# Gated units: the short chunk of the inner dimension in both halves of the rows, its product for four tiles on quarters of the array

## The chip, the cores and the metric

One Trainium2 chip, one of its cores. The metric is the device time of one execution in microseconds, median of several. A profiled execution, recorded by the hardware profiler, gives the trace that is read below. Engines: PE is TensorE (PEld its weight loads), DVE is VectorE, ACT is ScalarE, POOL is GpSimd, SP is the queue that issues most DMAs.

## The reference

Input x has 2 batches of 2048 tokens with 256 channels, all float32. Two blocks, each wrapped as `x + layernorm(block(layernorm(x)))`. The first is a sparse attention with compressed, selected and windowed parts. The second, which the change touches, is two layers of local attention, each followed by gated units:

```python
x = x + o @ wo                                    # after the local attention
h = shift_token(x)                                # second half of the channels from the token before
h = (h - mu) / jnp.sqrt(var + 1e-05) * lg + lb
h = h @ w1 + b1                                   # 256 -> 2 * 682
a, g = jnp.split(h, 2, axis=-1)
h = a * jax.nn.gelu(g, approximate=False)
x = x + h @ w2 + b2                               # 682 -> 256
```

The inner dimension is 682 = 5 * 128 + 42. After layer 1 comes the closing: layer norm of the result, plus the residual, to the output.

## The kernel before

Tokens are worked in tiles of 128; four tiles are a group (`GT = 4`), and there are eight groups, taken in the order `GORDER`. `Y[g]` holds a group's tokens in SBUF, `X[g]` the outer residual. The gated units of a layer are in `gated_units`. For each group:

- `shift` (DMA) makes the shifted half of the channels in `sh`; `moments` (DVE) and `deviations` (POOL) give mean and reciprocal deviation; `normed` (DVE) writes eight normalised 128x128 pieces into `hh`.
- `second_bias` adds b2 to the whole group on POOL, in place.
- `turned` (two of them, for the two halves of the channels) transposes four tiles on PE into a bank `pc`, and DVE writes them back with scale and bias as `hT`, also part of `hh`.
- `inner` multiplies one chunk c of the inner dimension for all four tiles: 512 columns, gate part into a bank `pg` and linear part into `pu`. The chunks 0 to 4 have 128 rows; chunk 5, the short one, has 42 (`REST`), and its gate and linear parts share one bank, gate rows at partitions 0 to 41 and linear rows at 64 to 105.
- `gate` applies Gelu on ACT into `ge`, and DVE multiplies into `u[:, c, :]`. There are two buffers u.
- `back` multiplies a tile's six chunks of u by w2 into a `pc` bank of 128x256 and adds it to Y on DVE. Chunk 5 is multiplied over all 128 rows; rows beyond 42 of u and w2 are zero.
- in the last layer `closing_moments` (DVE, then POOL for the reciprocal deviation r) and `closing_norm` (DVE norm to `res`, POOL adds X, SP stores) for each tile.

PSUM has 8 banks here, `share(ctx, "psum2", pa=2, pb=2, pc=4)`. A bank is reused in turn, when its last reader is done.

The order of the work is written by hand: `put(place, f, ...)` notes an operation with a place, and all are issued sorted by place, each engine taking its instructions in that order. `inner` of chunk c of the i-th group stands at (6 i + c) steps (`STEP`), so a place of 6 + k of a group is chunk k of the next one. `back` of tile k stands at 6 + k, `closing_moments` at 6.5 + k, `closing_norm` at 7.5 + k; `turned` at -2.1 and -1.1, that is in chunks 3.9 and 4.9 of the group before; `second_bias` at -2.5; `shift` at -9. So while a group's chunks are multiplied, the previous group's back products and the next group's norm and turns lie between them. A float32 product is two instructions in the trace. All of the gated units' instructions have the line of the recording helper, L124.

`Vectors.load` loads bias rows that are turned to columns (`col`); `load_gated` loads w1, w2 and b2 of a layer.

Of the kernel before, what the change touches and what calls it, by code (L numbers as in the profile page):

```python
# [12 lines left out]
AF = mybir.ActivationFunctionType  # L13
ALU = mybir.AluOpType
AX = mybir.AxisListType

P = 128
B, L, H = 2, 2048, 256
NT = L // P
GT = 4  # L20
# [4 lines left out]
HALF = 64  # L25
# [3 lines left out]
DEPTH, HEADS, DH = 2, 8, 64  # L29
INNER = HEADS * DH  # L30
HID = int(H * 4 * 2 / 3)
NCH = -(-HID // P)
FULL = (NCH - 1) * P
REST = HID - FULL
# [119 lines left out]
def sandwich_kernel(ctx: ExitStack, tc: tile.TileContext, x, Wq, bq, Wk, bk, Wv, bv, Wo, bo, Wg, bg,  # L154
                    Wc, bc, Ws, bs, wqkv, q_scale, k_scale, wo, ln_g, ln_b, w1, b1, w2, b2, rope, out):
    nc = Notes(tc.nc)
# [24 lines left out]
    def pc(shape):  # L181
        return bank("pc", shape)
# [10 lines left out]
    Y = [const.tile([P, GT, H], F32, tag=f"Y{g}", name=f"Y{g}") for g in range(B * NG)]  # L193
# [6 lines left out]
    def load(dst, src):  # L200
        nc.cut()
        nc.sync.dma_start(dst, src)
# [23 lines left out]
    cols = {}  # L226

    class Vectors:
# [10 lines left out]
        def load(self):  # L239
            if any(n % P for _, _, n in self.parts):  # L240
                nc.gpsimd.memset(self.row, 0.0)
            r = 0
            for _, src, n in self.parts:
                full = n // P
                load(self.row[r : r + full, :], src[0 : full * P].rearrange("(r p) -> r p", p=P))
                if n % P:
                    load(self.row[r + full : r + full + 1, 0 : n % P], src[full * P : n].unsqueeze(0))
                r += -(-n // P)

        def turn(self):  # L250
# [6 lines left out]
        (f"b1a{l}", b1[l, 0:HID], HID), (f"b1g{l}", b1[l, HID : 2 * HID], HID),  # L257
        (f"lg{l}", ln_g[l], H), (f"lb{l}", ln_b[l], H))])

    def col(name, i, n=P):  # L260
        return cols[name, i][:n]


    wpool = ctx.enter_context(tc.tile_pool(name="wpool", bufs=1))
# [33 lines left out]
    with part1 as s1:  # L298
# [403 lines left out]
        W = [dict() for _ in PAIRS]  # L702
# [186 lines left out]
    def load_gated(l):  # L889
        b2_b = wf.tile([P, H], F32, tag="b2", name=f"b2{l}")  # L890
        nc.gpsimd.dma_start(b2_b, b2[l].unsqueeze(0).to_broadcast([P, H]))


        a = wf.tile([P, 2, W1C], F32, tag="w1", name=f"w1{l}")
        w1v = w1[l].rearrange("(h p) n -> p h n", p=P)
        nc.gpsimd.memset(a[:, :, 2 * FULL :], 0.0)
        nc.sync.dma_start(a[:, :, 0:FULL], w1v[:, :, 0:FULL])
        nc.sync.dma_start(a[:, :, FULL : 2 * FULL], w1v[:, :, HID : HID + FULL])
        nc.sync.dma_start(a[:, :, 2 * FULL : 2 * FULL + REST], w1v[:, :, HID + FULL : 2 * HID])
        nc.sync.dma_start(a[:, :, 2 * FULL + HALF : 2 * FULL + HALF + REST], w1v[:, :, FULL:HID])  # L900
        o = wf.tile([P, NCH, H], F32, tag="w2", name=f"w2{l}")
        nc.gpsimd.memset(o[:, NCH - 1, :], 0.0)
        nc.sync.dma_start(o[:, 0 : NCH - 1, :], w2[l, 0:FULL, :].rearrange("(c p) n -> p c n", p=P))
        nc.sync.dma_start(o[0:REST, NCH - 1, :], w2[l, FULL:HID, :])
        return a, o, b2_b


# [6 lines left out]
    W = [dict() for _ in range(DEPTH)]  # L914
# [271 lines left out]
    GORDER = [b * NG + j for j in range(NG) for b in range(B)]  # L1186
# [6 lines left out]
    def gated_units(l, base, no_gate_until, beside):  # L1193
        G = {g: dict(u=U[i % 2]) for i, g in enumerate(GORDER)}

        def shift(g):

            s, y = G[g], Y[g]
            sh = act.tile([P, GT, P], F32, tag="oT", name="sh")
            if g % NG:  # L1200
                nc.sync.dma_start(sh[0:1, 0, :], G[g - 1]["kept"][P - 1 : P, :])
            else:
                nc.gpsimd.memset(sh[0:1, 0, :], 0.0)
            nc.sync.dma_start(sh[0:1, 1:GT, :], y[P - 1 : P, 0 : GT - 1, P:H])
            nc.sync.dma_start(sh[1:P, :, :], y[0 : P - 1, :, P:H])
            s["kept"] = act.tile([P, P], F32, tag="kept", name="kept", bufs=3)
            nc.gpsimd.tensor_copy(s["kept"], y[:, GT - 1, P:H])
            s["sh"] = sh

        def moments(g, k):  # L1210
            s = G[g]
            if k == 0:
                s["mv"] = small.tile([P, GT, 2], F32, tag="mv4", name="mv")
            stats(s["mv"][:, k, :], Y[g][:, k, 0:P], s["sh"][:, k, :])

        def deviations(g):
            G[g]["r"] = rstd_of(G[g]["mv"], GT, 1e-5)

        def normed(g, h, k):
            s = G[g]  # L1220
            if "hn" not in s:
                hh = act.tile([P, 2, 2 * GT * P], F32, tag="rr", name="hh")
                s["hn"] = hh[:, 0].rearrange("p (h k t) -> p h k t", h=2, k=GT)
                s["hT"] = hh[:, 1].rearrange("p (h t) -> p h t", h=2)
            norm(s["hn"][:, h, k, :], s["sh"][:, k, :] if h else Y[g][:, k, 0:P], s["mv"], k, s["r"])

        def second_bias(g):
            nc.gpsimd.tensor_tensor(Y[g], Y[g], W[l]["b2"].unsqueeze(1).to_broadcast([P, GT, H]), ALU.add)

        def turned(g, h):  # L1230
            s = G[g]
            pt = pc([P, GT, P])
            for k in range(GT):
                nc.tensor.transpose(pt[:, k, :], s["hn"][:, h, k, :], ident)
            nc.vector.tensor_scalar(s["hT"][:, h, :], pt.rearrange("p k t -> p (k t)"), col(f"lg{l}", h),
                                    col(f"lb{l}", h), ALU.mult, ALU.add)

        def inner(g, c, gate_bank, bank):
            s, w1_s = G[g], W[l]["w1"]

            def project(ps, lo):
                for h in range(2):
                    nc.tensor.matmul(ps, lhsT=w1_s[:, h, lo : lo + P], rhs=s["hT"][:, h, :],
                                     start=(h == 0), stop=(h == 1))

            pg = gate_bank([P, GT * P])
            if c < NCH - 1:
                pu = bank([P, GT * P])
                project(pg, FULL + c * P)
                project(pu, c * P)  # L1250
            else:
                pu = pg[HALF : HALF + REST]
                project(pg, 2 * FULL)
            s["in", c] = pg, pu

        def gate(g, c):
            s = G[g]
            pg, pu = s["in", c]
            n = P if c < NCH - 1 else REST
            ge = act.tile([P, GT * P], F32, tag="sq", name="ge")  # L1260
            nc.scalar.activation(ge[:n], pg[:n], AF.Gelu, bias=col(f"b1g{l}", c, n))
            nc.vector.scalar_tensor_tensor(s["u"][:n, c, :], pu[:n], col(f"b1a{l}", c, n), ge[:n],
                                           ALU.add, ALU.mult)

        def back(g, k):
            s, y = G[g], Y[g]
            pz = pc([P, H])
            for c in range(NCH):
                nc.tensor.matmul(pz, lhsT=s["u"][:, c, k * P : (k + 1) * P], rhs=W[l]["w2"][:, c, :],
                                 start=(c == 0), stop=(c == NCH - 1))  # L1270
            nc.vector.tensor_tensor(y[:, k, :], pz, y[:, k, :], ALU.add)

        def closing_moments(g, k):
            mv = small.tile([P, 1, 2], F32, tag="mv1", name="mv")
            stats(mv[:, 0, :], Y[g][:, k, :])
            G[g]["close", k] = mv, rstd_of(mv, 1, 1e-5)

        def closing_norm(g, k):
            res = act.tile([P, H], F32, tag="res", name="res")
            mv, r = G[g]["close", k]  # L1280
            norm(res, Y[g][:, k, :], mv, 0, r)
            nc.gpsimd.tensor_tensor(res, res, X[g][:, k, :], ALU.add)
            row = (g * GT + k) * P
            nc.sync.dma_start(of[row : row + P, :], res)


        plan = [(NCH + k, back, k) for k in range(GT)]
        plan += [(-9, shift), (-6, deviations), (-2.5, second_bias), (-2.1, turned, 0), (-1.1, turned, 1)]
        plan += [(-7 + 0.22 * k, moments, k) for k in range(GT)]
        plan += [(-4.5 + 0.22 * (h * GT + k), normed, h, k) for h in range(2) for k in range(GT)]  # L1290
        if l == DEPTH - 1:
            plan += [(NCH + k + 0.5, closing_moments, k) for k in range(GT)]
            plan += [(NCH + k + 1.5, closing_norm, k) for k in range(GT)]
        for i, g in enumerate(GORDER):
            for c in range(NCH):
                place = base + (NCH * i + c) * STEP
                put(place, inner, g, c, pc if place > beside else pa, pb if no_gate_until < place < beside else pc)
                put(max(place, no_gate_until) + 10, gate, g, c)
            for at, f, *arg in plan:
                put(base + (NCH * i + at) * STEP + 20, f, g, *arg)  # L1300

    def fetch(l, what):
# [75 lines left out]
```

## Time and profile before

| | us |
|---|---|
| median of 3 runs | 1618.66 (1618.02 to 1618.82) |
| profiled execution, its own time | 1617.42 |
| its span, first to last instruction | 1615.7 |
| PE busy | 1530.9 |
| DVE busy | 1068.0 |
| ACT busy | 757.3 |
| POOL busy | 733.5 |
| layer 0's gated units, about | 671 to 965 |
| layer 1's gated units, about | 1347 to 1612 |
| mean granted PE clock | 0.976 of full speed |

Times in the views are microseconds from the start of the span. A row of the timeline gives start, length, engine, line, operation, output and inputs, shape and count, and in brackets how long the engine had been idle and what released it. A row of the table of windows gives the stretch, its length, busy time of PE, PEld, DVE, ACT and POOL with instruction counts, the granted clock, the DMA share and GB/s.

### The profile page before, as it was taken

How to read it: one execution, taken by the hardware profiler on the slowest of the kernel's cores; microseconds unless marked ns; L12 is line 12 of the kernel's file. 1: busy time of each engine (PE TensorE's matmuls, PEld its weight loads, DVE VectorE, ACT ScalarE, POOL GpSimd, SP SyncE). 2: the span in 40 equal slices, each digit the busy share in tenths (PEclk: the TensorE clock that was granted, in tenths of full speed). 3: DMA queues.
4: the chain of work that ended last, by engine and by line, in shares of the span. 5: the costliest groups of instructions: out<-in, count | busy, mean ns of one | idle time of the engine just before them, and what ended most of it. 6: DMA issues, size and time to landing. Idle time of an engine off the chain costs nothing.

```text
span 1615.7 us, 32188 instructions
## 1 busy us (share of the span) xinstructions
PE 1530.9 (95%) x12216; PEld 1013.0 (63%) x12216; DVE 1068.0 (66%) x3123; ACT 757.3 (47%) x2197; POOL 733.5 (45%) x906
## 2 busy tenths in 40 slices
PE   7999957999999999789999999999999987999998
PEld 6867743666666666546566556666666664656655
DVE  6588673788888888544445247888888884455543
ACT  5236652677676776411111147677676763111110
POOL 7114255666666666301111156666666661132332
PEclk9999987999999999899999999999999998999999
DMA  6000002000000000020000010000000000000000
GB/s 213 1 4 4 1 2 80 8 5 8 6 8 9 5 7 7 8 68 7 10 20 0 1 39 28 9 5 9 5 8 8 9 4 9 11 25 28 27 26 26
DMA packets 32389, 30.66 MB, mean 19 GB/s; under 512 B 5118, under 2 KB 30572, under 8 KB 32236
## 3 DMA queue, kind: packets, MB, share of 16 engines
q1 hardware_dynamic: 32044, 28.08, 5.7%
q8 instruction: 97, 1.59, 0.4%
q0 software_dynamic: 192, 0.52, 0.2%
q14 instruction: 56, 0.46, 0.1%
HBM read 20.21 MB, written 4.19 MB: 15 GB/s over the span
## 4 chain that ended last, share of the span: by engine, by line
PE 87%; DVE 5%; POOL 3%; DMA 3%; ACT 1%; issue 1%; SPq 0%; POOLq 0%; DVEq 0%; ACTq 0%
PE pa L124 30%; PE pb L124 23%; PE pc L124 23%; PE pa L150 5%; PE pc L150 3%; DMA sh<-Y 2%; PE pb L150 2%; PE po L150 1%; DVE prob L124 1%; POOL rr L124 1%; DVE rr L124 1%; DVE st L150 1%; POOL r L150 1%; DMA cs<-in_rope_dram 0%; POOL ss L124 0%
## 5 line engine op out<-in xcount | busy, mean ns | idle before, releaser
L124 PE MATMUL pa<-wqkv,h 128*128 128x512 f32 x768 | 377.6, 615 | 19.3 <-ACT h L124 9.9
L124 POOL TENSOR_TENSOR rr<-rr 128x256 f32<-128x256 f32 x256 | 178.0, 727 | 305.8 <-DVE rr L124 259.4
L124 ACT ACTIVATE ge<-pa,vb 128x512 f32<-128x512 f32 x92 | 63.1, 688 | 365.7 <-PE pa L124 360.3
L124 ACT ACTIVATE prob<-prob,off 128x192 f32<-128x192 f32 (+2 forms) x512 | 226.2, 445 | 11.9 <-DVE off L124 11.0
L124 PEld LDWEIGHTS pa<-wqkv,h 128*128 128x128 f32 x768 | 133.9, 194 | 134.7 <-issue 107.7
L124 POOL TENSOR_TENSOR ss<-ss,mhalf 128x16 f32<-128x16 f32 x64 | 188.0, 2937 | 3.3 <-DVE den L124 2.3
L124 ACT COPY probT<-pb 128x384 f32<-128x384 f32 (+1 forms) x256 | 119.9, 469 | 142.6 <-PE pb L124 139.6
L124 PE MATMUL pa<-hh,w 128*128 128x512 f32 x368 | 176.4, 609 | 5.3 <-ACT ge L124 5.3
L124 PE MATMUL pc<-w,u 128*128 128x256 f32 x768 | 175.7, 379 | 0.0
L124 PEld LDWEIGHTS pc<-w,u 128*128 128x128 f32 x768 | 145.8, 190 | 45.4 <-issue 28.7
L124 DVE CUSTOM_DVE_ANT_0 prob<-pc,mask_loc 128x192 f32<-128x192 f32 (+2 forms) x512 | 148.7, 346 | 25.9 <-PE pc L124 24.1
L124 DVE TENSOR_TENSOR rr<-pa,cs 128x1024 f32<-128x1024 f32 x128 | 150.6, 1216 | 21.6 <-POOL cs L124 14.0
L124 PE MATMUL pb<-hh,w 128*128 128x512 f32 x292 | 137.7, 594 | 0.0
L124 POOL TENSOR_SCALAR r<-mv 128x1 f32<-128x1 f32 (+1 forms) x48 | 11.2, 233 | 274.9 <-DVE mv L124 274.9
L124 POOL TENSOR_TENSOR rr<-rr,ss 128x512 f32<-128x512 f32 x128 | 132.9, 1058 | 2.3
L124 DVE TENSOR_TENSOR prob<-prob,den 128x768 f32<-128x768 f32 x128 | 128.0, 1000 | 4.9
L124 PE MATMUL pb<-wo,oT 128*128 128x256 f32 x512 | 124.8, 388 | 5.8 <-DVE oT L124 5.8
L124 PEld LDWEIGHTS pb<-ident,prob 128*128 128x128 f32 x752 | 89.2, 141 | 65.4 <-DVE prob L124 27.7
L124 PE MATMUL pb<-ident,prob 128*128 128x128 f32 x752 | 118.3, 279 | 11.2 <-DVE prob L124 9.4
L124 DVE SCALAR_TENSOR_TENSOR u<-pb,vb,ge 128x512 f32<-128x512 f32 x73 | 54.7, 750 | 105.6 <-PE pb L124 79.8
L124 ACT ACTIVATE sq<-pa 128x512 f32<-128x512 f32 x128 | 75.9, 593 | 97.0 <-PE pa L124 94.2
L124 PE MATMUL pc<-kr,qT 64*64 64x192 f32 (+2 forms) x2688 | 111.1, 289 | 3.4 <-ACT qT L124 3.4
(255 smaller groups left out, 2498.6 us busy)
## 6 DMA issues: line engine op xcount, KB each, us to landing
cs<-in_rope_dram SPq DMA_DIRECT2D x32, 128.0 KB
out_dram<-res SPq DMA_DIRECT2D x32, 128.0 KB
sh<-Y SPq DMA_DIRECT2D x16, 254.0 KB
w<-in_L_ffn_w_dram SPq DMA_DIRECT2D x6, 640.0 KB
X<-_attn_hidden_states_dram SPq DMA_DIRECT2D x7, 512.0 KB
wqkv<-in_L_ffn_wqkv_dram SPq DMA_DIRECT2D x2, 1536.0 KB
Wc<-in_L_attn_Wc_dram SPq DMA_DIRECT2D x1, 1024.0 KB
wo<-in_L_ffn_wo_dram SPq DMA_DIRECT2D x2, 512.0 KB
```

Of the source, the lines that this page charges most:

```text
L124: return f(*a, **k)
L150: f(*(now(x) for x in a), **{n: now(x) for n, x in k.items()})
```

## The change

The short chunk of the inner dimension is stored in u with tiles 0 and 1 at partitions 0 to 63 and tiles 2 and 3 at 64 to 127, 256 columns each. Gelu and product of that chunk are done in two halves for it, one per pair of tiles. w2's short rows and the short bias are loaded twice, at partition 0 and at 64 (`HALF`). `back` multiplies only the five full chunks and leaves the sum in its bank. A new `back_rest` adds the short chunk: for each tile of a pair (j and j + 2) two products of 64 rows by 64 columns of weights and 256 columns of w2, each on its own quarter of the array. For the first six groups of a layer one `back_rest` serves all four tiles, after four `back`; for the last two there is one for tiles 0 and 2 and one for 1 and 3. `back_add`, the addition to Y, and the closing follow `back_rest`.

```diff
@@ Vectors.load
-                    load(self.row[r + full : r + full + 1, 0 : n % P], src[full * P : n].unsqueeze(0))
+                    nc.cut()
+                    for lo in (0, HALF):
+                        nc.sync.dma_start(self.row[r + full : r + full + 1, lo : lo + n % P], src[full * P : n].unsqueeze(0))
@@ load_gated
-        nc.sync.dma_start(o[0:REST, NCH - 1, :], w2[l, FULL:HID, :])
+        for lo in (0, HALF):
+            nc.sync.dma_start(o[lo : lo + REST, NCH - 1, :], w2[l, FULL:HID, :])
@@ gate
-            n = P if c < NCH - 1 else REST
             ge = act.tile([P, GT * P], F32, tag="sq", name="ge")
-            nc.scalar.activation(ge[:n], pg[:n], AF.Gelu, bias=col(f"b1g{l}", c, n))
-            nc.vector.scalar_tensor_tensor(s["u"][:n, c, :], pu[:n], col(f"b1a{l}", c, n), ge[:n],
-                                           ALU.add, ALU.mult)
+            parts = [(P, 0, 0, GT * P)] if c < NCH - 1 else [(REST, lo, lo // HALF * 2 * P, 2 * P) for lo in (0, HALF)]
+            for n, lo, t, m in parts:
+                nc.scalar.activation(ge[lo : lo + n, t : t + m], pg[:n, t : t + m], AF.Gelu, bias=col(f"b1g{l}", c, n))
+                nc.vector.scalar_tensor_tensor(s["u"][lo : lo + n, c, 0:m], pu[:n, t : t + m],
+                                               col(f"b1a{l}", c, n, lo), ge[lo : lo + n, t : t + m], ALU.add, ALU.mult)
@@ back
-            s, y = G[g], Y[g]
-            pz = pc([P, H])
-            for c in range(NCH):
-                nc.tensor.matmul(pz, lhsT=s["u"][:, c, k * P : (k + 1) * P], rhs=W[l]["w2"][:, c, :],
-                                 start=(c == 0), stop=(c == NCH - 1))
-            nc.vector.tensor_tensor(y[:, k, :], pz, y[:, k, :], ALU.add)
+            G[g]["z", k] = pz = pc([P, H])
+            for c in range(NCH - 1):
+                nc.tensor.matmul(pz, lhsT=G[g]["u"][:, c, k * P : (k + 1) * P], rhs=W[l]["w2"][:, c, :],
+                                 start=(c == 0), stop=False)
+
+        def back_rest(g, *pairs):
+            for j in pairs:
+                for i in range(2):
+                    rows = slice(i * HALF, (i + 1) * HALF)
+                    for half in range(2):
+                        t = j * P + half * HALF
+                        nc.tensor.matmul(G[g]["z", j + 2 * i][half * HALF : (half + 1) * HALF, :],
+                                         lhsT=G[g]["u"][rows, NCH - 1, t : t + HALF],
+                                         rhs=W[l]["w2"][rows, NCH - 1, :], start=False, stop=True)
+
+        def back_add(g, k):
+            y = Y[g][:, k, :]
+            nc.vector.tensor_tensor(y, G[g]["z", k], y, ALU.add)
@@ the plan
-        plan = [(NCH + k, back, k) for k in range(GT)]
+        plan = []
...
-        if l == DEPTH - 1:
-            plan += [(NCH + k + 0.5, closing_moments, k) for k in range(GT)]
-            plan += [(NCH + k + 1.5, closing_norm, k) for k in range(GT)]
+        def back_plan(fours):
+            at = NCH
+            for pairs in ((0, 1),) if fours else ((0,), (1,)):
+                tiles = [j + 2 * i for i in range(2) for j in pairs]
+                for n, k in enumerate(tiles):
+                    yield at + n, back, k
+                at += len(tiles)
+                yield at - 0.99, back_rest, *pairs
+                for n, k in enumerate(tiles):
+                    yield at - 0.98 + 0.1 * n, back_add, k
+                    if l == DEPTH - 1:
+                        yield at - 0.9 + 0.3 * n, closing_moments, k
+                        yield at - 0.6 + 0.3 * n, closing_norm, k
...
-            for at, f, *arg in plan:
+            for at, f, *arg in plan + list(back_plan(i < len(GORDER) - 2)):
```

More of the change, by code (lines that the diff above doesn't have):

```diff
@@ L258, in sandwich_kernel, with col @@
         (f"lg{l}", ln_g[l], H), (f"lb{l}", ln_b[l], H))])
-    def col(name, i, n=P):
-        return cols[name, i][:n]
+    def col(name, i, n=P, lo=0):
+        return cols[name, i][lo : lo + n]
     wpool = ctx.enter_context(tc.tile_pool(name="wpool", bufs=1))
```

## The prediction, made before the changed kernel was run

> **What bounds the kernel now.** I read the page first (sections 1 and 4), then one gated group in the table of windows, then the timeline of that group, row by row.
>
> ```profile
> span 1615.7 us, 32188 instructions
> PE 1530.9 (95%) x12216; PEld 1013.0 (63%) x12216; DVE 1068.0 (66%) x3123; ACT 757.3 (47%) x2197; POOL 733.5 (45%) x906
> PE 87%; DVE 5%; POOL 3%; DMA 3%; ACT 1%; issue 1%; SPq 0%; POOLq 0%; DVEq 0%; ACTq 0%
> ```
>
> TensorE is busy for 95% and carries 87% of the chain that ended last. In layer 1's gated units it has no gap: one group takes 30.12 us and PE is busy for all of it (columns after the colon: length, then busy PE, PEld, DVE, ACT, POOL, granted clock). The other engines are half idle, but VectorE works through its queue in order, so where its idle time lies matters.
>
> ```profile
> 1473.06:1503.18 30.12, 30.12 (x102) 18.26 (x101) 15.58 (x44) 4.13 (x6) 9.76 (x16) 1.00 0.09 27
> ```
>
> The place that the change touches, in layer 1: the last back product of a group, the two turns, the short chunk, the next group's first chunk.
>
> ```profile
> 1500.59 2.75 PE L124 MATMUL pc<-w,u 128*128 128x256 f32 x12
> 1503.18 0.60 PE L124 MATMUL pc<-ident,hh 128*128 128x128 f32 x4
> 1503.38 0.42 DVE L124 TENSOR_TENSOR Y<-pc,Y 128x256 f32<-128x256 f32 x1 [1.77 <-PE pc L124]
> 1504.53 0.40 DVE L124 TENSOR_SCALAR res<-Y,mv,r 128x256 f32<-128x256 f32 x1
> 1506.26 2.35 POOL L124 TENSOR_TENSOR Y<-Y,b 128x1024 f32<-128x1024 f32 x1
> 1507.49 3.60 PE L124 MATMUL pa<-hh,w 128*128 128x512 f32 x8
> 1507.99 0.78 DVE L124 TENSOR_SCALAR res<-Y,mv,r 128x256 f32<-128x256 f32 x1
> 1508.68 0.80 DVE L124 TENSOR_SCALAR hh<-pc,vb 128x512 f32<-128x512 f32 x1
> ```
>
> A product is two instructions. Twelve (six chunks) take 1500.59 to 1503.18 = 2.59 us, so a 128x256 product costs 0.431 us; 512 columns cost 0.86; a turn 0.44. The last row is turn 1's eviction into hh: done at 1509.48. The eight "pa" instructions from 1507.49 are the short chunk (1.72), then the next group's chunk 0; its second pair reads turn 1's half of hh at 1507.49 + 1.72 + 0.86 = 1510.07. So that eviction has 0.6 us to spare. This is the thin place.
>
> **What the change removes.** Per group, four short products of 0.431 = 1.72 us of PE time. In their stead: eight 64x64 products of 256 columns, two on each quarter. The attention's score products already run so:
>
> ```profile
> 404.55 0.83 PE L124 MATMUL pc<-kr,qT 64*64 64x192 f32 x16
> 405.31 0.55 PE L124 MATMUL pb<-ident,prob 128*128 128x128 f32 x3
> ```
>
> Sixteen instructions of 192 columns take 0.76 us to the next row; four per quarter at 192/256 of 0.2155 would be 0.65. The quarters run side by side and the block costs 0.11 more. For 256 columns: 4 x 0.2155 + 0.1 = 0.96. [...] I take the row, the same shape of tile on this chip. Gain: 0.76 per group of four, 0.86 - 0.53 = 0.33 per pair.
>
> **What it adds on PE.** pc has four buffers and back holds all four until back_add. Turn 0 follows back_rest directly and needs the first one. From the start of back_rest (t = 0): tile 0's quarters issue by 0.52, DVE starts 0.20 later (1503.18 to 1503.38), add 0.42, 0.1 back to PE (estimate): turn 0 at 1.24 instead of 0.96. Stall 0.28 (0 if hidden; 0.72 if tile 0 is only complete with the last quarter). Twelve groups of four have it.
>
> **What it moves on DVE and POOL, layer 1.** Today one closing (add, moments, norm) falls into each chunk. After it, in the built order, all four stand between chunk 3 and turn 1's eviction. DVE: add 0, hh, moments 0, adds 1 to 3, norm 0, moments 1, norm 1, moments 2, eviction of turn 0, u of chunk 4, norm 2, moments 3, norm 3, eviction of turn 1. POOL: r0, res0, r1, second_bias, res1, r2, res2, r3, res3. Norm k waits for r k; the tail of the trace shows what that round trip costs when nothing covers it:
>
> ```profile
> 1610.17 0.18 DVE L124 BATCH_NORM_AGGREGATE mv<-st 128x2 f32<-128x6 f32 x1
> 1610.44 0.28 POOL L124 TENSOR_SCALAR r<-mv 128x1 f32<-128x1 f32 x1 [0.99 <-DVE mv L124]
> 1610.80 0.55 POOL L124 TENSOR_TENSOR r<-r,mhalf 128x1 f32<-128x1 f32 x1
> 1611.39 0.80 DVE L124 TENSOR_SCALAR res<-Y,mv,r 128x256 f32<-128x256 f32 x1 [0.71 <-POOL r L124]
> ```
>
> Aggregate to norm: 1.22 us with POOL free (0.27, 0.36, 0.59). Other steps, start to start in these timelines: add to next add 0.34; stats to aggregate 0.46; norm to next 0.31 (0.69 beside second_bias); norm to POOL's res 0.49, res 0.69; second_bias 2.36; u 0.67-0.75.
>
> Walking both queues: add 0 at 0.72; aggregate 0 at 1.77, r0 usable at 2.99; adds to 2.9; norm 0 at 2.99; aggregate 1 at 3.76; POOL is in res0 until 4.17, so norm 1 at 5.12. POOL now runs second_bias 5.05 to 7.41, and res1 stands behind it, to 8.10. Aggregate 2 was at 6.27, but r2 starts at 8.10: norm 2 at 9.05 (eviction 0 and u fill the gap, from 6.37). Aggregate 3 at 9.82, res2 until 10.23, norm 3 at 11.18, eviction of turn 1 from 11.49 to 12.29, PE free at 12.39. PE wants it at 1.24 + 0.44 (turn 0) + 3.44 (chunk 4) + 0.44 (turn 1) + 1.72 (short chunk) + 0.86 = 8.14. **PE waits 4.25 us per group**, the main item. Bounds: 1.9 if second_bias came out of the way, 5.5 if POOL and DVE slow each other further. Behind it on DVE stand the short chunk's two u and the next moments; their readers are 4 us or more away. u of chunk 4 (7.1) frees its pb bank early enough.
>
> **What the wait does to the clock.** Waits of this size were followed by half speed:
>
> ```profile
> 687.45 3.41 PE L124 MATMUL pa<-hh,w 128*128 128x512 f32 x4 [2.65 <-ACT ge L124]
> 684.80:687.45 2.65, 0.00 (x1) 0.01 (x1) 0.02 (x1) 2.63 (x7) 0.00 (x0) 1.00 0.01 1
> 687.90:691.30 3.40, 3.40 (x5) 1.35 (x4) 1.19 (x3) 0.48 (x2) 0.00 (x0) 0.50 0.06 17
> ```
>
> After 2.65 us of idle PE the granted clock is 0.50 for 3.4 us, which costs 1.7 us. Of eight gaps of 2.6 to 3.8 us around both starts of the gated units seven were followed by such a stretch. [...] The rows decide: 1.5 per group, 9.0 in all; both ends kept.
>
> **At nothing.** Gate's short chunk becomes two ACT and two DVE instructions of 256 columns, by the neighbouring forms (a 384-column copy 469 ns, a 512-column one 587; a 256-column product-and-add 484) about 0.2 us more on each: ACT idles 3 us before it and readers in back_rest come three chunks later; on the path, 0.4 a group. Four more 42-element bias loads stand on SP where the next loads wait 207 us for another buffer; the second copy of 42 rows of w2 (43 KB per layer) lands tens of us before the first back product. Uncovered: 0.5 us each by the row of a small sh load. SP's sh loads now stand behind norm 3's output rather than norm 1's; they are needed a period later.
>
> **Sum.** Layer 1, six groups of four: -0.76 + 0.28 + 4.25 = +3.77, so +22.6; clock +9.0. Layer 0, six groups (no closings, so only the stall): -0.48 each, -2.9. Pairs: -0.66 for group 6 of layer 1; -1.3 for two groups in layer 0, less 0.5 because chunk 4 of its last group takes a bank that back_add has yet to free: -0.8. Tail: -0.66 on PE, but two closings follow the last product: last res 5.0 us after it instead of 3.24: +1.1. Total +28.3. The profiled execution took 1617.42 (1.7 around its span); 1645.7 against it, 1647 against the median, 1.24 higher.
>
> **Rivals.** *Evictions in time, faster.* If DVE and POOL get through the closings by 8.1, only gains and the 0.28 stalls remain: 12 x -0.48, pairs -2.1, tail +1.75: -6, 1612.5. It decides where the wait is under 1.0 us a group with no clock loss. For it: DVE is busy 15.6 of 30.1 us. Against: in-order queue, 0.6 us of room, second_bias in front of res1. 8%.
> *Half the wait.* second_bias finds a free POOL earlier, or closings overlap better: 1.9 us wait, no slow clock: 6 x 1.4 - 2.9 - 0.4 = +5, 1624; with some clock loss up to 1632. 14%.
> *Quarters in turn.* The blocks don't run side by side (all four write with start off): no gain, 0.86 more in twelve groups, and a later add: +28 + 14 = 1661. Against: the attention's products accumulate so too. 8%.
> *The main case*, 1632 to 1660: 70%. The lower end is the wait without clock loss and a smaller eviction delay, the upper one two slow stretches per wait.
>
> Range 1624 to 1661. Chances: faster 0.08, within 0.2% 0.03, slower 0.89; 0.2% (3 us) is about what a measurement of this kernel can tell from no change.
>
> **What would show it.** Period of layer 1's gated groups near 35.4 us (30.12 + 3.77 + 1.5), of layer 0's near 29.6; PE waits of about 4 us before "pa<-hh,w" put down to DVE hh, six times; granted clock below 1.00 there; norms waiting for POOL r; second_bias between r1 and res1; quarter blocks of about 0.96 us with 64*64 tiles. I am wrong if eviction 1 ends within 8 us of back_rest's start, or if the quarter blocks take 1.7 us or more.

## The result, and the profile after

| | before | after |
|---|---|---|
| median, us | 1618.34 (1615.83 to 1618.82) | 1654.37 (1650.39 to 1656.02) |
| ratio after to before, 95% interval | | 1.0221 (1.0202 to 1.0239) |
| profiled execution's span, us | 1615.7 | 1652.5 |
| mean granted PE clock | 0.976 | 0.967 |

The changed kernel is 36 us slower. Among the runs of the experiments below, one of e3 (2638.69 us) and one of e4 (4016.25 us) were in a slow state; their medians are of the others. The page of after, with the span, the engines and the shares of the chain that ended last:

```profile
span 1652.5 us, 32512 instructions
PE 1539.6 (93%) x12344; PEld 999.8 (61%) x12344; DVE 1081.9 (65%) x3139; ACT 758.9 (46%) x2213; POOL 734.0 (44%) x906
PE 73%; DVE 5%; DMA 2%; POOL 2%; issue 1%; ACT 1%; POOLq 0%; SPq 0%; DVEq 0%; ACTq 0%
```

TensorE's share of the chain fell from 87% to 73%, although it is busy for longer than before (1539.6 us for 1530.9): part of its work runs at a lower clock (the granted mean is 0.967 for 0.976). Its waits (what it waited for, total us, times, longest) have a row that before has not:

```profile
PE pa L124 <- DVE hh L124: 24.5, 12, 2.7
```

Twelve waits for VectorE's `hh`: two in each of the six groups of four in layer 1. In the table of windows, first a whole period of layer 1, then one of layer 0, which has no closings; then, in another group of layer 1, its two waits and the half-speed stretch:

```profile
1482.22:1519.58 37.36, 33.19 (x110) 18.28 (x109) 17.48 (x46) 4.37 (x7) 9.61 (x16) 0.91 0.07 22
794.67:824.39 29.72, 29.64 (x108) 17.21 (x109) 14.03 (x34) 4.37 (x7) 3.84 (x4) 1.00 0.04 10
1450.80:1452.22 1.42, 0.00 (x0) 0.03 (x1) 1.39 (x5) 0.47 (x1) 1.14 (x3) 1.00 0.00 0
1453.32:1455.99 2.67, 0.00 (x1) 0.01 (x1) 1.41 (x5) 0.00 (x0) 1.98 (x4) 0.81 0.15 49
1455.00:1461.80 6.80, 5.81 (x8) 2.63 (x9) 4.49 (x17) 1.15 (x2) 2.18 (x4) 0.50 0.10 31
```

Layer 0's period went from 30.12 to 29.72 us. Layer 1's went from 30.12 to 36.75 (mean of five: 36.83, 37.18, 37.36, 35.75, 36.65). In it PE stands idle for 1.42 + 2.67 us, and afterwards, in the group shown, has 5.81 us of work at half speed, which costs half of that, 2.9 (four instructions of 512 columns take 3.41 us there, 1457.86 to 1461.27, and 1.72 at a clock of 1.00, 1446.76 to 1448.48). Five of the six groups have a stretch of 6.8 us at half speed, one has 3.4; PE works through 5.06, 5.79, 6.16, 2.94, 4.73 and 5.64 us of them, so that the first five, whose periods these are, lose 2.5 on average.

The timeline of one group of layer 1 in after, from its last full chunks to the second half of the next group's chunk 0 (in brackets: idle time before, and what ended it):

```profile
1478.30 3.35 PE L124 MATMUL pc<-w,u 128*128 128x256 f32 x26
1481.25 0.42 DVE L124 TENSOR_TENSOR Y<-pc,Y 128x256 f32<-128x256 f32 x1 [1.93 <-PE pc L124]
1481.73 0.66 PE L124 MATMUL pc<-ident,hh 128*128 128x128 f32 x4
...
1485.51 2.35 POOL L124 TENSOR_TENSOR Y<-Y,b 128x1024 f32<-128x1024 f32 x1
1485.57 2.43 DVE L124 TENSOR_SCALAR res<-Y,mv,r 128x256 f32<-128x256 f32 x1 [1.19 <-POOL r L124]
1488.08 0.72 POOL L124 TENSOR_TENSOR res<-res,X 128x256 f32<-128x256 f32 x1 [0.23 <-DVE res L124]
1488.47 0.78 DVE L124 TENSOR_SCALAR hh<-pc,vb 128x512 f32<-128x512 f32 x1
1489.39 1.10 PE L124 MATMUL pa<-hh,w 128*128 128x512 f32 x2 [1.42 <-DVE hh L124]
1491.97 0.41 DVE L124 TENSOR_SCALAR res<-Y,mv,r 128x256 f32<-128x256 f32 x1 [1.19 <-POOL r L124]
1492.30 0.81 DVE L124 TENSOR_SCALAR hh<-pc,vb 128x512 f32<-128x512 f32 x1
1493.16 2.08 PE L124 MATMUL pa<-hh,w 128*128 128x512 f32 x2 [2.67 <-DVE hh L124]
1493.66 0.47 ACT L124 ACTIVATE ge<-pa,vb 42x256 f32<-42x256 f32 x1 [5.17 <-DVE u L124]
```

The block of quarters ends at 1481.73, where the turn starts. VectorE's norm of the second tile starts at 1485.57 beside `second_bias` on GpSimd and takes 2.43 us, to 1488.00, just after `second_bias` is done (1487.86). Behind it in VectorE's queue stands turn 0's eviction into `hh` (1488.47, though the turn's row ends at 1482.39), and the next group's first product waits for that. Norm 3 (1491.97) comes late because everything behind norm 1 on VectorE, and res1 and r2 behind `second_bias` on GpSimd, came late; turn 1's eviction (1492.30) stands behind norm 3, and PE waits a second time. The last row is a wait that nobody feels: ScalarE's second half of the short chunk waits for VectorE's first half (both halves lie in one `ge` tile, which is probably why); the rows that read u come three chunks later.

Theory A, from these rows: the loss comes from the closings, which the change has bunched on VectorE and GpSimd in front of the turns' evictions, with `second_bias` in their middle, and from the low clock that follows PE's waits. The quarters themselves gain. Theory B: the quarters, or the four banks of `pc` held until the block is done, are a cost of their own, in which the short chunk's halves have a part.

### The profile page after: what moved, and what is told of

The parts are those of the page before. It is cut to its first block, busy times and chain, and to the rows that moved or that the text cites. A ratio compares the mean times of both kernels' runs of the same rounds, so it can differ in the third digit from the quotient of the medians.

```text
span 1652.5 us, 32512 instructions
## 1 busy us (share of the span) xinstructions
PE 1539.6 (93%) x12344; PEld 999.8 (61%) x12344; DVE 1081.9 (65%) x3139; ACT 758.9 (46%) x2213; POOL 734.0 (44%) x906
## 4 chain that ended last, share of the span: by engine, by line
PE 73%; DVE 5%; DMA 2%; POOL 2%; issue 1%; ACT 1%; POOLq 0%; SPq 0%; DVEq 0%; ACTq 0%
PE pa L124 28%; PE pb L124 23%; PE pc L124 21%; DMA sh<-Y 2%; DVE res L124 1%; DVE prob L124 1%; DVE Y L124 1%; DVE hh L124 1%; POOL r L124 1%; POOL res L124 1%; DVE rr L124 0%; DVE u L124 0%; POOL rr L124 0%; DVE st L124 0%; DVE ss L124 0%
## 5 line engine op out<-in xcount | busy, mean ns | idle before, releaser
L124 PE MATMUL pa<-wqkv,h 128*128 128x512 f32 x768 | 373.4, 609 | 20.3 <-ACT h L124 10.1
L124 ACT ACTIVATE ge<-pa,vb 128x512 f32<-128x512 f32 (+1 forms) x107 | 66.7, 625 | 401.8 <-PE pa L124 322.1
L124 PE MATMUL pa<-hh,w 128*128 128x512 f32 x368 | 186.3, 632 | 29.8 <-DVE hh L124 24.5
L124 PE MATMUL pc<-w,u 128*128 128x256 f32 (+1 forms) x896 | 166.2, 384 | 0.0
L124 PEld LDWEIGHTS pc<-w,u 128*128 128x128 f32 (+1 forms) x896 | 130.9, 175 | 52.9 <-issue 38.1
L124 PE MATMUL pb<-hh,w 128*128 128x512 f32 x292 | 146.8, 628 | 0.0
L124 PEld LDWEIGHTS pa<-hh,w 128*128 128x128 f32 x368 | 68.5, 198 | 90.6 <-issue 48.1
```

Source lines behind the costliest of these rows:

```text
L124: return f(*a, **k)
```

## The experiments

All ran on one chip, the first four beside a before of 1614.13 us, the last three beside a before of 1614.8. Ratios are to before, with a 95% interval.

**e1: the quarters, with the closings spread again**

```diff
-                        yield at - 0.9 + 0.3 * n, closing_moments, k
-                        yield at - 0.6 + 0.3 * n, closing_norm, k
+                        late, step = (0.5, 1) if fours else (-0.9, 0.3)
+                        yield at + late + step * n, closing_moments, k
+                        yield at + late + step * n + (1 if fours else 0.3), closing_norm, k
```

> The changed kernel, with the closings of the first six groups of layer 1 put one to a chunk from chunk 4 on (moments at 10.5 + n, norm at 11.5 + n) instead of all after back_rest. Theory (closings on VectorE and GpSimd stand in front of the turns' evictions): TensorE's waits for hh are gone, no slow clock in layer 1's steady part, period there 29.7 us as in layer 0, total 1610 to 1614. Rival (the four held pc banks and the quarter blocks cost the time): period stays near 37, total near 1650.

Measured: 1609.48 us, ratio 0.9971 (0.9958 to 0.9985). A period of layer 1, then the block and the turn behind it in the timeline, then the quarters' row in the groups by form (engine, operation, tile, count, busy us, mean ns, idle before):

```profile
1469.37:1499.10 29.73, 29.64 (x109) 17.18 (x109) 15.91 (x46) 4.37 (x7) 9.76 (x16) 1.00 0.09 28
```

```profile
1465.94 3.35 PE L124 MATMUL pc<-w,u 128*128 128x256 f32 x26
1469.37 0.66 PE L124 MATMUL pc<-ident,hh 128*128 128x128 f32 x4
```

```profile
L124 PE MATMUL pc<-w,u 64*64 64x256 f32 x64 | 4.4, 389 | 0.0
```

The same quarters, banks and halves of the short chunk, and layer 1 runs at 29.73 us, clock 1.00, without a wait (the total is half a microsecond below the 1610 to 1614 that were expected). So moving the closings alone turns a loss of 2.2% into a gain of 0.3%. With the closings out of GpSimd's queue, `second_bias` too runs earlier, ahead of the block (1463.24 to 1465.58); e2 takes the two apart. B's cost, if any, is smaller than what the quarters save. (In the last row the instructions overlap: 64 of 389 ns each are busy for 4.4 us together, so 389 ns is the length of one, not its price.)

**e2: the change, with `second_bias` issued before the closings**

```diff
-        plan += [(-9, shift), (-6, deviations), (-2.5, second_bias), (-2.1, turned, 0), (-1.1, turned, 1)]
+        plan += [(-9, shift), (-6, deviations), (-3.2, second_bias), (-2.1, turned, 0), (-1.1, turned, 1)]
```

> The changed kernel, with second_bias at place -3.2 instead of -2.5, so that GpSimd has done it before the closings begin. Theory: half of the wait is GpSimd's: by the same walk turn 1's eviction ends near 10.7 instead of 12, TensorE waits 2 to 2.6 us instead of 4.5, total 1630 to 1643 depending on whether the clock still falls. Rival (second_bias holding VectorE off is the whole cause): waits gone, total 1610 to 1616. Second rival (banks and quarters): no change, 1650 to 1656.

Measured: 1641.3 us, ratio 1.0182 (1.0165 to 1.0199). Waits of PE; `second_bias` and the norms of `hh` that now stand beside it; norm 1 and the products after the wait; then windows of the wait, of the half-speed stretch and of a whole period:

```profile
PE pa L124 <- DVE hh L124: 14.0, 6, 2.3
```

```profile
1472.33 2.88 DVE L124 TENSOR_SCALAR hh<-sh,mv,r 128x128 f32<-128x128 f32 x3
1472.49 2.38 POOL L124 TENSOR_TENSOR Y<-Y,b 128x1024 f32<-128x1024 f32 x1 [11.50 <-DVE hh L124]
1484.02 0.41 DVE L124 TENSOR_SCALAR res<-Y,mv,r 128x256 f32<-128x256 f32 x1 [1.20 <-POOL r L124]
1489.60 1.63 PE L124 MATMUL pa<-hh,w 128*128 128x512 f32 x2 [2.34 <-DVE hh L124]
```

```profile
1487.26:1489.60 2.34, 0.00 (x2) 0.00 (x1) 1.16 (x3) 0.00 (x0) 1.65 (x4) 1.00 0.17 56
1490.10:1493.50 3.40, 3.40 (x5) 1.35 (x4) 2.73 (x13) 1.15 (x2) 0.00 (x0) 0.50 0.16 46
1480.16:1514.18 34.02, 31.60 (x109) 17.68 (x109) 17.51 (x46) 4.37 (x7) 9.69 (x16) 0.95 0.08 24
```

Norm 1 takes 0.41 us where it meets no `second_bias`, and turn 0's eviction is in time again: the first wait is gone in all six groups. (`second_bias` now stands beside three norms of `hh`, which take 2.88 us together where three take 0.85 in e3, at 1484.89, but eight microseconds ahead of the closings, and PE does not wait there.) The second stays, at 2.32 to 2.34, and in the group shown 3.40 us at half speed follow it. Behind each of the six, the first six instructions of 512 columns take 4.37 or 4.38 us, start to start, for the 2.58 (6 x 0.43) that six take at full speed. 29.73 + 2.34 + 1.70 = 33.8, of 34.02 measured; the missing 0.25 comes with the wait (see the sum of a period below). So `second_bias` in the middle is the smaller part; four closings ahead of the evictions are enough for a loss of 1.8%.

**e3: the change, with the turns' evictions on ScalarE**

```diff
-            nc.vector.tensor_scalar(s["hT"][:, h, :], pt.rearrange("p k t -> p (k t)"), col(f"lg{l}", h),
-                                    col(f"lb{l}", h), ALU.mult, ALU.add)
+            nc.scalar.activation(s["hT"][:, h, :], pt.rearrange("p k t -> p (k t)"), AF.Identity,
+                                 bias=col(f"lb{l}", h), scale=col(f"lg{l}", h))
```

> The changed kernel, with both turns' evictions (scale and bias into hT) on ScalarE instead of VectorE, in both layers; the closings stay bunched. Theory: TensorE no longer waits for VectorE there, total 1612 to 1620 (a remaining wait of up to 1 us a group where the short chunk's u, still behind the closings, frees its bank late). Rival (banks and quarters): 1650 to 1656.

Measured: 1616.30 us, ratio 1.0017 (1.0008 to 1.0026). From its timeline:

```profile
1472.00 2.43 DVE L124 TENSOR_SCALAR res<-Y,mv,r 128x256 f32<-128x256 f32 x1 [1.20 <-POOL r L124]
1472.71 0.78 ACT L124 ACTIVATE hh<-pc,vb 128x512 f32<-128x512 f32 x1 [1.47 <-PE pc L124]
1480.45 1.95 PE L124 MATMUL pa<-hh,w 128*128 128x512 f32 x4 [0.46 <-DVE u L124]
```

The closings are as bunched as in after, norm 1 still takes its 2.43 us, and yet only 0.17% of after's 2.21% is left, because the evictions no longer stand behind it. What is left is one wait of 0.46 us a group, for the short chunk's bank, which VectorE reads late (`DVE u`). No half-speed stretch follows that wait: the clock is 1.00 over the whole period from 1450.00 to 1480.42, and the four instructions behind each of the six waits (0.45 to 0.48) have a row of 1.95 or 1.96 us, for 1.88 elsewhere. The period is 30.42 us, 0.69 more than in e1: the 0.46, and 0.23 that come with a wait (see the sum of a period below). Over six groups that is 4.1 of the 6.8 us by which e3 is behind e1. The rest was not followed up; the turns of layer 0 are on ScalarE too in this kernel.

**e4: the kernel before, with the closings bunched.** No quarters, no halves; the closings of the first six groups stand at the places where the change puts them.

```diff
-            plan += [(NCH + k + 0.5, closing_moments, k) for k in range(GT)]
-            plan += [(NCH + k + 1.5, closing_norm, k) for k in range(GT)]
+                    m, n = (NCH + 3.1 + 0.3 * k, NCH + 3.4 + 0.3 * k) if four else (NCH + k + 0.5, NCH + k + 1.5)
+                    closing += [(m, closing_moments, k), (n, closing_norm, k)]
```

> The kernel before (full 128-row products, add after each tile), with only the closings of the first six groups of layer 1 moved to the places that the change gives them (moments at 9.1 + 0.3 n, norm at 9.4 + 0.3 n). Theory: the loss is here without any quarter: waits of 3.5 to 4.5 us for hh and a slow clock, total 1648 to 1660. Rival (banks and quarters): stays at 1618.

Measured: 1660.48 us, ratio 1.0295 (1.0275 to 1.0316). Waits, one period, and the timeline of a group:

```profile
PE pa L124 <- DVE hh L124: 28.7, 12, 2.7
```

```profile
1490.44:1527.93 37.49, 32.67 (x102) 18.89 (x100) 17.50 (x44) 4.12 (x6) 9.60 (x16) 0.91 0.07 21
```

```profile
1491.02 2.34 POOL L124 TENSOR_TENSOR Y<-Y,b 128x1024 f32<-128x1024 f32 x1
1491.09 2.42 DVE L124 TENSOR_SCALAR res<-Y,mv,r 128x256 f32<-128x256 f32 x1 [1.19 <-POOL r L124]
1494.91 1.10 PE L124 MATMUL pa<-hh,w 128*128 128x512 f32 x2 [2.15 <-DVE hh L124]
1498.67 2.08 PE L124 MATMUL pa<-hh,w 128*128 128x512 f32 x2 [2.67 <-DVE hh L124]
```

The whole loss without a single quarter, a little more than expected (the two waits together are 4.8 us): norm 1 of 2.42 us beside `second_bias`, two waits a group, the clock at 0.91 over the period. Its period is 37.46 us in the mean of five, 0.71 more than after's: 0.73 because the first wait is 2.15 us rather than 1.42, 0.40 because the quarters' gain is missing, less about 0.4 because PE does less work at half speed (4.16 to 4.40 us a group). With e1 this settles it from both sides: bunching alone loses 2.9%, quarters alone gain 0.3%.

**e5: e1, with halves of the rows in place of quarters**

```diff
-                    for half in range(2):
-                        t = j * P + half * HALF
-                        nc.tensor.matmul(G[g]["z", j + 2 * i][half * HALF : (half + 1) * HALF, :],
-                                         lhsT=G[g]["u"][rows, NCH - 1, t : t + HALF],
-                                         rhs=W[l]["w2"][rows, NCH - 1, :], start=False, stop=True)
+                    nc.tensor.matmul(G[g]["z", j + 2 * i], lhsT=G[g]["u"][rows, NCH - 1, j * P : (j + 1) * P],
+                                     rhs=W[l]["w2"][rows, NCH - 1, :], start=False, stop=True)
```

> The changed kernel with the closings spread one to a chunk, and the short product on halves of the array instead of quarters: each tile's short chunk is one product of 64 rows by 128 columns of weights, two tiles side by side on the two halves of the rows, four products in a group instead of eight. If the two halves run side by side as the quarters do: block again about 0.95 us (0.86 and the change of tiling), time as with quarters, 0.997 of the kernel before. If halves don't overlap: 1.8 us a block, 12 x 0.86 more, near or above the kernel before.

Measured: 1612.32 us, ratio 0.9981 (0.9974 to 0.9988), period of layer 1 29.76 us. The products' row by form:

```profile
L124 PE MATMUL pc<-w,u 64*128 64x256 f32 x32 | 4.5, 402 | 0.0
```

Half as many instructions, each as long as a quarter's (402 ns for 389), and the same period within 0.03 us: two products of 64x128 run side by side as four of 64x64 do. Splitting the columns as well brings nothing here. (The total is above the 0.997 that was expected, but its interval overlaps that of e1.)

**e6: e1, with turn 0 after chunk 4, so that it finds a free bank**

```diff
-        plan += [(-9, shift), (-6, deviations), (-2.5, second_bias), (-2.1, turned, 0), (-1.1, turned, 1)]
+        plan += [(-9, shift), (-6, deviations), (-2.5, second_bias), (-1.9, turned, 0), (-1.1, turned, 1)]
```

> The changed kernel with the closings spread, and turn 0 at place -1.9 instead of -2.1, so that chunk 4's four products stand between back_rest and the turn. Theory: the 0.25 us in which the turn waits for the first pc bank (block start to turn 1.27 us, of it 0.93 us quarters) is covered, twelve groups, 3 us less than with the closings spread alone: 0.995 to 0.996 of the kernel before. Rival (the time after the block is the array's change of tiling, not the bank): no difference, 0.997.

Measured: 1612.08 us, ratio 0.9982 (0.9973 to 0.9991), period 29.61 us. Its block, and the chunk that now follows it:

```profile
1433.28 3.35 PE L124 MATMUL pc<-w,u 128*128 128x256 f32 x26
1436.55 0.70 PE L124 MATMUL pa<-hh,w 128*128 128x512 f32 x1
```

The 26 instructions of the first row are ten full ones, at 0.431/2 each, and the 16 of the block. Ten take 2.155 of the 3.27 us to the next row, so the block with both changes of tiling takes 1.11 us. Worked out in the same way it takes 1.27 in after, up to the turn (1443.28 to 1444.55 in one group). The period is 0.11 us shorter than e1's, where a stall of 0.25 had been expected to go. Over twelve groups 0.11 is 1.3 us, below what the totals can tell: in them e6 and e1 cannot be told apart, and the expectation of 0.995 to 0.996 was missed. So the bank's wait is 0.11 (by the period) to 0.16 us (by the block), of the 0.28 at which I had put it, and the rest lies in the block.

**e7: e5 and e6 together**

> Both: row halves and turn 0 after chunk 4. If halves equal quarters, as with turn 0 moved alone, 0.995 to 0.996.

Measured: 1609.82 us, ratio 0.9969 (0.9959 to 0.9979), period 29.65 us. The expectation of 0.995 to 0.996 was missed here too. e1, e5, e6 and e7 all run a little faster than both kernels; between the four the intervals overlap, and I rank none of them.

## Why the prediction was right, and where its terms were off

The direction and the mechanism were right: 1647 predicted, 1654.37 measured; +28.3 us of sum, +36.8 between the two spans. The walk of the queues held within 0.1 us up to the start of norm 1 (5.12 walked, 5.11 measured) and missed how long that norm takes. The terms, with what stands in their place:

- **Period of layer 0** (−0.48 predicted): −0.40. Of the 0.08 that are missing, 0.03 are in the block with its stall, which takes 1.27 us for 1.24; the other 0.05 were not followed up. (The 0.1 back to PE in my walk was an estimate with no row behind it; in after tile 0's addition ends at 1481.67 and the turn starts at 1481.73, 0.06.) The split was off more than the sum: e6 gives 1.11 for the block and 0.16 for the bank, not 0.96 and 0.28. The row of the attention's score products misled me: ahead of it stand products on 64x64 tiles too (first row below), so it holds only one change of tiling. The same sixteen instructions between two 128x128 stretches take 400.37 − 399.56 = 0.81 us, not 0.76:

```profile
403.16 1.57 PE L124 MATMUL pc<-probT,v 64*64 64x128 f32 x64
399.56 0.88 PE L124 MATMUL pc<-kr,qT 64*64 64x192 f32 x16
400.37 1.98 PE L124 MATMUL pa<-wqkv,h 128*128 128x512 f32 x4
```

From the last two rows the block would have been 0.86 + 0.16 (0.81 less 0.65) = 1.02, an estimate of mine. The 1.11 of e6 is counted from the full products ahead of the block, and the 1.02 from the block's own first instruction. That it is the change of tiling which costs what the block takes beyond 0.86 was my reading of the rows, and no run shows it by itself.
- **PE's wait in layer 1** (4.25 a group predicted, all of it at turn 1's eviction): 1.42 + 2.67 = 4.09 us of idle time, at two places. The step that failed is norm 1. I costed it at 0.69 beside `second_bias`, from the row of before in which such a norm took 0.78; it takes 2.43 (2.42 in e4), and 0.41 with `second_bias` out of the way (e2). In before the norm merely began near the end of `second_bias`: 1507.99 + 0.78 = 1508.77, while `second_bias` ended at 1506.26 + 2.35 = 1508.61. In after, too, the norm ends 0.14 us after `second_bias` does. In all six cases of before and all six of after such a norm ended 0.13 to 0.16 us after `second_bias`, whether it had begun 0.06 us into it or 1.74. So did the one shown of e3 (1474.43 for 1474.27) and the one of e4 (1493.51 for 1493.36). Read so, the row of before already showed a norm that ends when GpSimd has finished, and not one that is slowed by a fixed amount: beside `second_bias` it has 0.78 us or 2.43, by its start, and 0.41 without it. What holds it the traces do not show. With a norm of 2.43 us turn 0's eviction comes at 8.0 us after the block's start (1480.46 to 1488.47) and not at the 6.4 that I had walked to: the first wait. Turn 1's eviction came at 11.8, where I had 11.5. What PE waits in all is set by that last eviction, and the first wait only takes a part of it earlier; so the sum changed little, and that 4.25 was so near is in part luck.
- **The clock after the wait** (1.5 a group predicted): 1.5 to 3.1, 15.2 us in the six groups for 9.0 (half of the 30.3 us of work listed above). This is the largest miss, 6.2 us of the total. One wait of 2.34 us is followed by 3.40 us at half speed in e2, as the rows of before had it. The size was right for one wait, but there are two waits, 1.1 us of work apart, and in five groups of six 6.8 us at half speed behind them. No single wait in these groups is longer than 2.67 us. The trace of after shows where such stretches begin: at 1417.40, 1454.95, 1492.50, 1530.04, 1564.18 and 1601.72, which lie 37.5 or 34.1 us apart, 11 or 10 times 3.41; they last 6.83 us, one of them 3.41. So here they begin a whole number of times 3.41 us from one another, and 0.6 to 2.2 us into the second wait. Cut into pieces of 3.41 us from such a start, the group with two half-speed pieces and the one with a single piece read:

```profile
1451.54:1454.95 3.41, 1.10 (x2) 0.30 (x2) 2.18 (x6) 0.00 (x0) 2.29 (x6) 1.00 0.20 65
1454.95:1458.36 3.41, 2.37 (x3) 1.18 (x4) 2.78 (x9) 0.67 (x2) 0.72 (x1) 0.50 0.17 55
1458.36:1461.77 3.41, 3.41 (x6) 1.43 (x5) 1.74 (x10) 0.49 (x1) 1.46 (x3) 0.50 0.05 12
1526.63:1530.04 3.41, 1.10 (x2) 0.30 (x2) 2.19 (x6) 0.00 (x0) 2.12 (x5) 1.00 0.23 77
1530.04:1533.46 3.42, 2.94 (x4) 1.40 (x5) 2.75 (x11) 1.15 (x2) 0.51 (x1) 0.50 0.12 39
1533.46:1536.87 3.41, 3.41 (x14) 2.44 (x14) 1.76 (x7) 0.00 (x0) 1.46 (x3) 1.00 0.06 15
```

In both groups a piece with 2.31 us of idle PE (3.41 − 1.10) was followed by one at half speed. In the first that one had 1.04 us of idle time and a second followed; in the other it had 0.48 and none did. In the six groups of after the pieces at full speed that half speed followed had 1.99 to 2.31 us of idle time, the half-speed pieces that another followed 0.66 to 2.1, while a piece at full speed with 1.29 us (1523.22 to 1526.63) was followed by full speed. The prediction's eighth gap, the one that no half speed followed (1362.73 to 1365.38 in before), has such a point in it, 1363.70, three times 3.41 us ahead of the half speed that begins at 1373.94: 0.97 us of it lie before that point and 1.68 behind. These rows give no limit: elsewhere in after half speed followed a piece with 1.44 us of idle time (212.50 to 215.91) and did not follow one with 1.92 (1338.89 to 1342.30).
- **The sum of a period**: the two terms above leave a rest. In each of the five periods 29.72 + 4.09 and that group's own half-speed loss fall short of the measured period by 0.47 us; in e2, with one wait a group, 0.25 are missing, in e3 0.23. So a wait costs about 0.24 us beyond its idle time, and the two of a group 4.56 in all, for the 4.25 predicted. (A part of it is how a row's end is drawn: four instructions of 512 columns have a row of 1.88 us, but the next row starts 1.72 us after their start, 1482.22 to 1483.94 in after.) With it the sum is 30.12 − 0.40 + 4.09 + 0.47 + 2.47 = 36.75, the mean measured. Predicted: 35.4.
- **From the start to layer 1's first block** (−4.2 predicted: −2.9, −0.8 for the pairs, −0.5): the turn behind that block starts at 1407.72 in after and at 1412.81 in before, −5.1. In e1, which does the same up to there, it is at 1409.93; two executions differ by 2 us in this part, so the term is right as far as these traces can tell.
- **From the turn behind the sixth block to the end**: 61.0 us in after (1591.49 to 1652.5), 53.7 in e1 (1558.54 to 1612.2), 52.3 in before (1563.42 to 1615.7). So 7.3 are the sixth group's waits and slow clock (4.07 + 0.47 + 2.82 = 7.4), and pairs and tail together cost 1.4, where I had +0.4 (−0.66 and +1.1). The last addition of X starts 4.7 us after the last product's row ends, for 3.1 before, 1.6 more, so the tail itself was no worse than I had it (1.8 more); the missing microsecond lies in the two pair groups and was not followed up. In all: −5.1 + 5 x 6.63 + 7.3 + 1.4 = 36.8.
- **Rivals.** "Evictions in time" is what e1 shows, with the closings elsewhere: 0.9971 of before is 1613.6 against the first median, where I had 1612.5. As a forecast for this change it fell. "Quarters in turn" is excluded by e1's and e5's periods: had the quarters run one behind the other, the block would have taken 8 x 0.431 = 3.45 us, twice the 1.72 of the full products, and a period would have been longer than 30.12. (By this the rival's own sum, with 0.86 more in a block, was too small.) "Half the wait" is close to what e2 builds by hand, but with the slow clock that I had left out of its lower half.

## What to carry to other kernels

A change that makes several results come ready at once moves everything that hangs on them too: write out the queue of each engine behind the spot, since the work that moved here (closings on VectorE and GpSimd) had nothing to do with what was sped up (TensorE), and cost 2.5% of the time (after against e1), where the products had saved 0.3%. When a row shows an instruction longer than usual beside another engine's, compare the two ends before taking its length as a price: if it ends when the other ends, as the norm here did, its length depends on where it began (2.43 us begun at 0.06, 0.77 at 1.73). And price a short wait of TensorE with the half-speed stretch behind it: here one wait of 2.34 us cost 1.7 more by the clock (e2), two of 1.42 and 2.67 close together 2.5 on average (after).

## What the hardware showed that I had not expected

- A VectorE norm (SBUF to SBUF, 128x256, float32) that starts 0.06 us after a GpSimd addition of 128x1024 took 2.43 us in place of 0.41, and ended 0.14 us behind it (after, 1488.00 for 1487.86). A VectorE product that reads PSUM (u, 128x512) ran inside the same addition in before in 0.75 us (1507.32, in an addition from 1506.26 to 1508.61), the mean of all 73 of that form.
- A PE gap of 2.34 us was followed by 3.40 us at half speed, and the six gaps of that size by the same slow products, 4.37 us for 2.58 (e2); gaps of 0.46 were not (e3); two gaps of 1.4 and 2.7 us with 1.1 of work between them were followed by 6.8 us, in five groups of six (after). In the six groups of after these stretches begin 10 or 11 times 3.41 us apart, each behind a piece of 3.41 us with 1.99 to 2.31 us of idle time in it.
- Two products of 64 rows by 128 columns on the two halves of the rows cost a period the same as four of 64 by 64 on quarters (29.76 us for 29.73). The block of 16 quarter instructions with both changes of tiling took 1.11 us, for 1.72 us of full products.
